# Round three of a graph network: each tile finished inside the loop of sums

## The chip, the cores and the metric

The kernel runs on one core of a Trainium2 chip. The metric is the device time of one execution in microseconds (us), smaller is better. The core has a matrix engine (PE; its weight loads are listed as PEld), a vector engine (DVE), a scalar engine (ACT), a general engine that here issues gathers and scatters (POOL) and a queue engine that issues DMA transfers (SP). Each engine works through its own list of instructions in order; between engines, semaphores make an instruction wait for what it reads.

## The reference, cut to what matters

A residual network of eight layers acts on 3125 nodes with 256 features. Each layer adds its output to x, and each reads the layer norm of x. The change lies in the third round, a weighted graph convolution with a two-layer product behind it, and in the preparation of the mixture layer that follows, whose gate is an attention over another graph of 65536 edges:

```python
# round three, graph layer (sums over the first graph, self-loops included)
xw = layernorm(x) @ W
h7 = segment_sum(xw[col] * (dinv[row] * ew * dinv[col])[:, None], row) + b
x = x + relu(h7 @ W1 + b1) @ W2 + b2
# round three, mixture layer: scores of the gate, over the other graph
h = layernorm(x) @ W_gat                      # 4 heads of 4 values
a_src, a_dst = (h * att_src).sum(-1), (h * att_dst).sum(-1)
# attention over the other graph's edges, norm, the best 2 of 4 experts
...
x = x + sum over experts of gate * (gelu(layernorm(x) @ W1[e] + b1[e]) @ W2[e] + b2[e])
```

## The kernel before

The nodes are 25 tiles of 128 rows (`T` = 25, `D` = 256, `DC` = 2 halves of the features, `TG` = 5 tiles to a group). The rounds follow one another; this document is about the stretch from the end of round two's mixture to the first gather of round three's attention.

`r2_gnn` (L1010) norms all tiles, transposes them (`moe_input`, L672, `tr_ps`), multiplies by W and scales by `dv` (`r_p`, `r_xw`), then calls `src_sum` (L2334). That is the loop this document calls **the loop of sums**. In its iteration t one matrix `ss_wt` of 1.6 MB is loaded from memory and 25 products are summed in `ss_sum` for tile t (L2360; each f32 product is two PE instructions, so 50 instructions). Beside the sums, the loop puts the other graph's edges in order, block by block. `own_order` (L1791) is a generator with five steps; the steps of block b are called here S1 to S5:

- S1: ACT makes a one-hot matrix `oo_h` (17 Abs, L1801, and one Relu, L1802).
- S2: DVE adds it up and scans it (`oo_hs`, `oo_sm`, `oo_ls`).
- S3: PE makes two small products (`oo_p`, L1826, L1827); DVE works out places (`oo_m`, `oo_pos`, `oo_eq`, `oo_pi`, `oo_pf`, L1831 to L1849); ACT makes a second one-hot `oo_hp` from `oo_pf` (again 17 Abs and a Relu); DVE makes `oo_hk`, `oo_rh` (L1855, L1859).
- S4: PE multiplies `oo_hp` with `oo_rh` (L1864, 17 instructions).
- S5: DVE writes the ordered block into `own_gi` and `own_rel` (L1867 to L1869).

Iteration t runs S1(t), S3(t-1), S4(t-2), the sums of tile t, S5(t-2), `done(t-1)` (two DVE operations on `r_acc`, L1040, L1041), S2(t). All of it stands under `self.in_order(nc.tensor, nc.vector, nc.scalar)` (L1920): PE, DVE and ACT each execute their instructions of the loop strictly in the order in which the program emits them. SP, POOL and everything outside such a block are ordered by the planner.

After the loop, `own_marks` (L1872) marks first and last edges for all 25 blocks at once (`mark_edges`, L1628: per block a copy, a PE transpose and a cast, then four transposes and transfers into `relT`); all 25 `r_acc` tiles are transposed; the two-layer product runs over four tiles at a time (`r_a`, L1058, Relu on ACT, `r_o`, L1065) and is added to `self.X` with the bias b2 (L1067, L1068). Then `r2_ffn` (L2367) loads the gate's weights (`head_weights`, L1905), norms x (`norm_group`, L145), transposes it (`tr_ps`), multiplies by the gate's weights (`q_hp`, L2409), copies (`q_hx`, L2411) and writes the rows `q_rows` to memory; the attention's POOL gathers (`ad_rows`, L322) read them.

Of the kernel before, what the change touches and what calls it, by code (L numbers as in the profile page):

```python
# [36 lines left out]
NP = T * P  # L37
D = 256
DC = D // P
# [4 lines left out]
TG = 5  # L44
# [1113 lines left out]
class Fast(Net):  # L1158
# [469 lines left out]
    def mark_edges(self, s, first, pool, p2, psp):  # L1628

        nc, K = self.nc, s.K  # L1630
        nc.vector.tensor_scalar(s.neg, s.rel, float(P), -BIG, op0=OP.is_ge, op1=OP.mult)
# [3 lines left out]
        for k in s.k0:  # L1635
            nc.vector.memset(go[:, k:k + 1], 0.0)
        st = pool.tile([P, K], F32, name="te_st")
        nc.vector.tensor_tensor_scan(st, go, first, 0.0, OP.mult, OP.max)
        nc.vector.tensor_scalar_mul(s.cum, st, -BIG)
        nc.vector.tensor_scalar(go, go, -1.0, 1.0, op0=OP.mult, op1=OP.add)  # L1640
        nc.vector.tensor_max(go, go, first)
        nc.vector.tensor_scalar_mul(s.drop, go, -BIG)
# [8 lines left out]
        for k in range(0, K, W):  # L1651
            ps = psp.tile([P, P], F32, name="te_pr")[0:W, :]
            nc.tensor.transpose(ps, s.rel[:, k:k + W], self.ident)
            r = p2.tile([W, P], BF16, name="te_r")
            nc.vector.tensor_copy(r, ps)
            nc.sync.dma_start(s.relT[k:k + W, :], r)
# [90 lines left out]
    def own_load(self):  # L1747
# [6 lines left out]
        self.edge_tiles(s, keep, "own", self.d.rec.rearrange("p k f -> p (k f)"))  # L1754
        s.low = keep.tile([P, KB, KB], BF16, name="own_low")
# [116 lines left out]
    def own_marks(self):  # L1872

        nc, tc, s = self.nc, self.tc, self.o
        K = s.K
        with tc.tile_pool(name="om", bufs=1) as pool, tc.tile_pool(name="om2", bufs=2) as p2, \
                tc.tile_pool(name="om_ps", bufs=2, space=PSUM) as psp:
            n = KB * (T - 1)
            ends = pool.tile([P, 2, T], F32, name="om_ends")
            full = s.rel1[:, 0:n].rearrange("p (d k) -> p d k", k=KB)  # L1880
            for i, (u, v) in enumerate(((KB - 1, KL - 1), (0, 0))):
                nc.vector.tensor_copy(ends[:, i, 0:T - 1], full[:, :, u])
                nc.vector.tensor_copy(ends[:, i, T - 1:T], s.rel1[:, n + v:n + v + 1])
            near = pool.tile([P, 2, P], F32, name="om_near")
            nc.vector.memset(near, 0.0)
            nc.vector.tensor_copy(near[:, 0, 1:P], self.ident[:, 0:P - 1])
            nc.vector.tensor_copy(near[:, 1, 0:P - 1], self.ident[:, 1:P])
            first = pool.tile([P, K], F32, name="om_first")
            ps = psp.tile([P, 2, T], F32, name="om_p")
            for i in range(2):  # L1890
                nc.tensor.matmul(ps[:, i, :], near[:, i, :], ends[:, i, :], start=True, stop=True)
            r, f, l = s.rel1, first, s.last
            nc.vector.tensor_tensor(f[:, 1:K], r[:, 1:K], r[:, 0:K - 1], OP.not_equal)
            nc.vector.tensor_tensor(l[:, 0:K - 1], r[:, 0:K - 1], r[:, 1:K], OP.not_equal)
            nc.vector.tensor_tensor(f[:, 0:n].rearrange("p (d k) -> p d k", k=KB)[:, :, 0], full[:, :, 0], ps[:, 0, 0:T - 1], OP.not_equal)
            nc.vector.tensor_tensor(l[:, 0:n].rearrange("p (d k) -> p d k", k=KB)[:, :, KB - 1], full[:, :, KB - 1],
                                    ps[:, 1, 0:T - 1], OP.not_equal)
            nc.vector.tensor_tensor(f[:, n:n + 1], r[:, n:n + 1], ps[:, 0, T - 1:T], OP.not_equal)
            nc.vector.tensor_tensor(l[:, K - 1:K], r[:, K - 1:K], ps[:, 1, T - 1:T], OP.not_equal)
            no = pool.tile([P, K], F32, name="om_no")  # L1900
            nc.vector.tensor_scalar(no, r, 0.0, 256.0, op0=OP.is_equal, op1=OP.mult)
            nc.vector.scalar_tensor_tensor(s.rel, r, -1.0, no, op0=OP.add, op1=OP.add)
            self.mark_edges(s, first, pool, p2, psp)
# [430 lines left out]
    def src_sum(self, rows, done):  # L2334


        nc, tc = self.nc, self.tc
        self.own_load()
        with tc.tile_pool(name="ss_w", bufs=2) as wp, tc.tile_pool(name="ss_ps", bufs=2, space=PSUM) as psp, \
                tc.tile_pool(name="oo", bufs=2) as op, tc.tile_pool(name="oo1", bufs=1) as o1, \  # L2340
                tc.tile_pool(name="oo_ps", bufs=1, space=PSUM) as osp, \
                self.in_order(nc.tensor, nc.vector, nc.scalar):
            ways, sums = {}, {}

            def step(b):
                if b in ways:
                    next(ways[b])

            for t in range(T + 2):
                if t < T:  # L2350
                    ways[t] = self.own_order(t, op, o1, osp)
                step(t)
                step(t - 1)
                step(t - 2)
                if t < T:
                    wt = wp.tile([P, T, P], F32, name="ss_wt")
                    nc.sync.dma_start(wt, self.mats[:, t, :, :])
                    sums[t] = psp.tile([P, D], F32, name="ss_sum")
                    for d in range(T):
                        nc.tensor.matmul(sums[t], wt[:, d, :], rows[:, d, :], start=d == 0, stop=d == T - 1)  # L2360
                step(t - 2)
                if t - 1 in sums:
                    done(t - 1, sums[t - 1])
                step(t)
        self.own_marks()

    def r2_ffn(self):  # L2367
# [7 lines left out]
        with ExitStack() as ctx:  # L2375
            pool = ctx.enter_context(tc.tile_pool(name="q", bufs=1))
# [17 lines left out]
            for e in range(1, E):  # L2394
                nc.vector.memset(early[:, e, 0:e], 1.0)
            we = self.head_weights(pool, a["L2_ffn_W_gat"], a["L2_ffn_att_src"].rearrange("h c -> (h c)"),
                                   a["L2_ffn_att_dst"].rearrange("h c -> (h c)"), C=4)
            xT = self.moe_input(pool)
            hx = pool.tile([P, T, Q + 4], F32, name="q_hx")
            ad = pool.tile([P, T, 4], F32, name="q_ad")  # L2400
            sf = pool.tile([P, T, 4], F32, name="q_sf")
            rows = self.dram.tile([NP, Q + 4], F32, name="q_rows")
            with tc.tile_pool(name="q_ps", bufs=2, space=PSUM) as psp:
                for g in range(0, T, TG):
                    gs = slice(g, g + TG)
# [166 lines left out]
```

## Time and profile before

| | us |
|---|---|
| median of 3 runs | 5167.04 (5164.95 to 5167.39) |
| profiled execution, its time | 5171.12 |
| profiled execution, its span | 5169.1 |
| busy in the span: PE, DVE, ACT, POOL | 3584.2, 2916.1, 2087.0, 2063.2 |
| first product of the loop of sums to the last tile's sums | 2690.93 to about 3049 |
| first gather of round three's attention | 3217.24 |

The page of the profile lists busy times of each engine, the chain of work that ended last, and groups of instructions with their mean durations. Times inside the span are counted from its start. A line of a timeline gives start, duration, engine, source line, operation, output and inputs, how many instructions were merged, and in brackets how long the engine sat idle before it and what released it.

### The profile page before, as it was taken

The page shows a single profiled execution, that of the slowest core. Times are in us where ns is not written, and L with a number is a line of the kernel's source. Part 1 is how long each engine was busy: PE and PEld are TensorE (multiplying, and loading weights), DVE is VectorE, ACT ScalarE, POOL GpSimd, SP SyncE. Part 2 cuts the span into 40 slices and gives each one's busy share as a digit, 9 for nine tenths or more (in the row PEclk, how much of TensorE's full clock was granted, in tenths as well). Part 3 has the DMA queues.
Part 4 walks back from the last instruction along what each step waited for, and adds up shares of the span by engine and source line. Part 5 has one row for each costly group of instructions (what it writes and reads, how often), then busy time and mean ns, then how long its engine had stood idle before and what let it go on. Part 6 is the DMA issues. An engine that isn't in the chain of part 4 may idle for free.

```text
span 5169.1 us, 67040 instructions
## 1 busy us (share of the span) xinstructions
PE 3584.2 (69%) x21332; PEld 2847.3 (55%) x21332; DVE 2916.1 (56%) x9571; ACT 2087.0 (40%) x5715; POOL 2063.2 (40%) x2082
## 2 busy tenths in 40 slices
PE   1399969625666354554648876168786999979994
PEld 1399958524444243443537754035554788868883
DVE  7998842255666466663358874577747872231112
ACT  3466432116666467661129961023232331112220
POOL 0365443467776677775620000777700000120003
PEclk9699979866777677777969986578887999989997
DMA  1632237534554344434723311111100112225554
GB/s 55 206 109 103 99 123 234 174 89 136 142 142 125 97 133 130 135 99 132 205 74 115 115 57 45 34 31 35 33 1 25 68 68 76 92 103 193 193 192 135
DMA packets 345199, 562.37 MB, mean 109 GB/s; under 512 B 69987, under 2 KB 255719, under 8 KB 341637
## 3 DMA queue, kind: packets, MB, share of 16 engines
q1 hardware_dynamic: 229050, 373.88, 21.8%
q0 software_dynamic: 84032, 154.27, 11.7%
q10 hardware_dynamic: 31754, 29.84, 1.7%
q8 instruction: 172, 2.82, 0.2%
q14 instruction: 191, 1.56, 0.1%
HBM read 412.89 MB, written 145.37 MB: 108 GB/s over the span
## 4 chain that ended last, share of the span: by engine, by line
PE 44%; POOL 11%; DVE 9%; ACT 9%; issue 8%; DMA 5%; SPq 1%; DVEq 0%; ACTq 0%; POOLq 0%
POOL ad_rows L322 9%; PE gx_pa L962 7%; PE r_pa L1581 7%; PE gx_po L933 7%; PE ad_acc L2133 6%; ACT oo_y L1801 4%; PE q_a L2484 3%; PE q_o L2492 3%; PE r_o L1596 2%; DMA ad_rows<-r_rows,fa_gi 1%; DMA gb_y<-ff_results,gd_at 1%; ACT ad_rows L2123 1%; ACT oo_hp L1802 1%; ACT oo_h L1802 1%; DMA gx_xs<-regions 1%
## 5 line engine op out<-in xcount | busy, mean ns | idle before, releaser
L322 POOL DMA_INDIRECT ad_rows<-r_rows,fa_gi x832 | 823.3, 990 | 266.4 <-issue 241.3
L1737 POOL DMA_INDIRECT os_table<-os_rec,os_at x512 | 531.1, 1037 | 526.2 <-ACT gx_h L963 194.0
L322 POOL DMA_INDIRECT ad_rows<-q_rows,own_gi x416 | 402.6, 968 | 719.9 <-DMA q_rows<-q_hx 593.4
L2123 ACT ACTIVATE ad_rows<-ad_rows 128x64 f32<-128x64 f32 x2544 | 617.0, 334 | 1.6
L2133 PE MATMUL ad_acc<-ad_rows,ad_hd 128*128 128x260 f32 x1664 | 515.9, 464 | 3.3 <-ACT ad_rows L2123 2.4
L831 POOL DMA_INDIRECT regions<-gh_xn,gd_at x150 | 157.5, 1050 | 845.7 <-PE r_o L1596 624.4
L1581 PE MATMUL r_pa<-r_xs,r_cnt 128*128 128x257 bf16 x3750 | 467.7, 277 | 28.1 <-DVE r_xs L1357 14.2
L963 ACT ACTIVATE gx_h<-gx_pa,gx_bias 128x256 f32<-128x256 f32 x448 | 211.9, 473 | 671.2 <-PE gx_pa L962 642.6
L935 DVE TENSOR_TENSOR gx_ys<-gx_po,gx_b 128x256 f32<-128x256 f32 x192 | 80.6, 423 | 622.1 <-PE gx_po L933 600.8
L962 PE MATMUL gx_pa<-gx_xt,gx_w 128*128 128x256 f32 x1792 | 418.5, 388 | 6.8 <-DMA gx_w<-in_L_ffn_W 3.2
L933 PE MATMUL gx_po<-gx_w,gx_h 128*128 128x256 f32 x1792 | 419.5, 380 | 0.0
L1581 PEld LDWEIGHTS <-r_cnt 128*128 128x128 bf16 x3750 | 365.0, 99 | 84.9 <-issue 29.4
L2133 PEld LDWEIGHTS ad_acc<-ad_rows,ad_hd 128*128 128x128 f32 x1664 | 365.8, 232 | 68.9 <-ACT ad_rows L2123 5.4
L2036 PE MATMUL ad_pt<-ident,ad_e 128*4 128x128 f32 x75 | 26.6, 354 | 525.9 <-DVE ad_e L2033 396.0
L962 PEld LDWEIGHTS gx_pa<-gx_xt,gx_w 128*128 128x128 f32 x1792 | 336.6, 192 | 81.7 <-DVE gx_xt L957 21.5
L933 PEld LDWEIGHTS gx_po<-gx_w,gx_h 128*128 128x128 f32 x1792 | 331.2, 190 | 44.0 <-ACT gx_h L963 2.6
L322 POOL DMA_INDIRECT gb_y<-ff_results,gd_at x150 | 144.3, 962 | 526.9 <-DMA ff_results<-gx_ys 476.1
L2036 PEld LDWEIGHTS ad_pt<-ident,ad_e 128*4 128x4 f32 x75 | 6.1, 82 | 559.1 <-issue 527.4
L1462 PE MATMUL r_pa<-r_xn,r_wt 128*128 128x257 f32 x1250 | 298.1, 383 | 7.2 <-ACT r_wt L1497 5.9
L2360 PE MATMUL ss_sum<-r_xw,ss_wt 128*128 128x256 f32 x1250 | 292.0, 396 | 6.3 <-DMA ss_wt<-mats 6.3
L2360 PEld LDWEIGHTS ss_sum<-r_xw,ss_wt 128*128 128x128 f32 x1250 | 246.9, 199 | 42.3 <-issue 6.7
L1462 PEld LDWEIGHTS r_pa<-r_xn,r_wt 128*128 128x128 f32 x1250 | 228.4, 192 | 35.5 <-ACT r_wt L1497 6.5
(555 smaller groups left out, 6920.6 us busy)
## 6 DMA issues: line engine op xcount, KB each, us to landing
gx_w<-in_L_ffn_W SPq DMA_DIRECT2D x64, 1024.0 KB
mats<-r_wt SPq DMA_DIRECT2D x25, 1600.0 KB
ss_wt<-mats SPq DMA_DIRECT2D x25, 1600.0 KB
gx_w<-in_L_ffn_W SPq DMA_DIRECT2D x64, 512.0 KB
regions<-zero SPq DMA_DIRECT2D x26, 1024.0 KB
ad_rb<-fa_relT SPq DMA_DIRECT2D x48, 544.0 KB
gx_xs<-regions SPq DMA_DIRECT2D x96, 256.0 KB
ff_results<-gx_ys ACTq DMA_DIRECT2D x96, 256.0 KB
```

Of the source, the lines that this page charges most:

```text
L322: return self.nc.gpsimd.indirect_dma_start(out=out, out_offset=None, in_=table[:, :], in_offset=bass.IndirectOffsetOnAxis(ap=idx, axis=0))
L831: ins = nc.gpsimd.indirect_dma_start(out=self.regions[:, :], out_offset=bass.IndirectOffsetOnAxis(ap=m.at[i][:, t:t + 1], axis=0), in_=x, ...
L933: nc.tensor.matmul(po, h[:, f, j * P:(j + 1) * P], w2s[:, f, :], start=f == 0, stop=f == FC - 1)
L962: nc.tensor.matmul(ps, w1s[:, c, f * P:(f + 1) * P], xt[:, c, :], start=c == 0, stop=c == DC - 1)
L963: done = nc.scalar.activation(h[:, f, :], ps, act, bias=bias1[:, f, k:k + 1])
L1462: nc.tensor.matmul(pa, wt[:, i, :], xn[:, g * G + i, :], start=i == 0, stop=i == G - 1)
L1581: nc.tensor.matmul(pa, c[:, u, :], xs[i - 1][:, u, j, :], start=u == 0 and j == 0, stop=u == T - 1 and j == 2)
L1737: i = nc.gpsimd.indirect_dma_start(out=s.table[:, :], out_offset=bass.IndirectOffsetOnAxis(ap=s.at[:, c:c + 1], axis=0), in_=s.rec[:, c, : ...
L1801: nc.scalar.activation(y[:, k, :], self.iotab, AF.Abs, bias=minus[:, k:k + 1])
L2123: i = nc.scalar.activation(v, v, AF.Copy, scale=x.rt[:, k, W4 + h:W4 + h + 1])
L2133: nc.tensor.matmul(x.acc, lhs[:, k, :], rhs[:, k, :], start=i == 0, stop=i == x.kb - 1)
L2360: nc.tensor.matmul(sums[t], wt[:, d, :], rows[:, d, :], start=d == 0, stop=d == T - 1)
```

## The change

`src_sum` is merged into a new `r2_gnn`. Behind the sums of a tile, the rest of that tile's work is put into the same loop, under the same fixed order, as generators in a list `later`; `on()` moves each of them one step, in list order. It is called twice in an iteration: before the sums of tile t and behind them. In this document the steps are F1, F2, F3 for `finish` (transposes and copy; first product and Relu; second product and add), M1 and M2 for `own_marks` of five blocks, and N, B1, B2, B3, Q for `scores` of five tiles (norm; three batches of transposes; scores, copy and transfer; its first step is empty).

The loop's new PSUM tiles are: `te_pr` in one buffer (marks), `lt_pt` in two (all transposes and the first product), `lt_po` in one (the second product and the scores). The start of the round also changes: tile by tile it transposes, copies on ACT, multiplies by W and scales; the gate's weights are loaded there; b2 is added to X by 25 POOL operations. `r2_ffn` loses its norm, transposes and scores.

```diff
-    def mark_edges(self, s, first, pool, p2, psp):
+    def mark_edges(self, s, first, pool, p2, psp, b0=0, b1=T):
...
-        for b in range(T):
+        for b in range(b0, b1):
             e = p2.tile([P, 4], F32, name="te_e")
             k = s.k0[b] + s.kb[b] - 1
             nc.vector.tensor_copy(e, s.cum[:, k:k + 1].to_broadcast([P, 4]))
...
             nc.tensor.transpose(ps, e, self.ident)
             nc.vector.tensor_copy(s.dropT[:, b, :], ps)
...
-    def own_marks(self):
+    def own_marks(self, pool, p2, psp, near, b0, b1):
...
+        for i, (u, v) in enumerate(((KB - 1, KL - 1), (0, 0))):
+            nc.vector.tensor_copy(ends[:, i, 0:full], wide[:, :, u])
...
+        for i in range(2):
+            nc.tensor.matmul(ps[:, i, 0:n], near[:, i, :], ends[:, i, 0:n], start=True, stop=True)
+        nc.vector.tensor_tensor(f[:, 1:K], r[:, 1:K], r[:, 0:K - 1], OP.not_equal)
...
+        yield
+        self.mark_edges(s, f, pool, p2, psp, b0, b1)
...
+                for g in range(0, T, TG):
+                    xn = xp.tile([P, TG, D], F32, name="r2_xn")
+                    self.norm_group(lp, xn, g)
+                    for t in range(TG):
...
+                        nc.scalar.copy(xt, pt)
...
+                            nc.tensor.matmul(ps, xt[:, c, :], w[:, c, :], start=c == 0, stop=c == DC - 1)
+                        nc.vector.tensor_scalar_mul(xw[:, g + t, :], ps, dv[:, g + t:g + t + 1])
+                    for t in range(g, g + TG):
+                        nc.gpsimd.tensor_add(self.X[:, t, :], self.X[:, t, :], b2)
...
+                    tc.tile_pool(name="om_ps", bufs=1, space=PSUM) as mps, \
...
+                    tc.tile_pool(name="lt_ps", bufs=2, space=PSUM) as bank, \
+                    tc.tile_pool(name="lt_po", bufs=1, space=PSUM) as one, \
+                    self.in_order(nc.tensor, nc.vector, nc.scalar):
...
+                def finish(t, total):
+                    acc = tp.tile([P, D], F32, name="lt_acc")
+                    nc.vector.tensor_add(acc, total, xw[:, t, :])
+                    nc.vector.scalar_tensor_tensor(acc, acc, dv[:, t:t + 1], b, op0=OP.mult, op1=OP.add)
+                    yield
...
+                        nc.tensor.transpose(pt[:, c, :], acc[:, c * P:(c + 1) * P], self.ident)
+                    at = tp.tile([P, DC, P], F32, name="lt_at")
+                    nc.scalar.copy(at, pt)
+                    yield
...
+                            nc.tensor.matmul(ph[:, f, :], w1[:, c, f * P:(f + 1) * P], at[:, c, :], start=c == 0, stop=c == DC - 1)
+                    for f in range(DC):
+                        nc.scalar.activation(h[:, f, :], ph[:, f, :], AF.Relu, bias=b1[:, f:f + 1])
+                    yield
+                    po = one.tile([P, D], F32, name="lt_po")
+                    for f in range(DC):
+                        nc.tensor.matmul(po, h[:, f, :], w2[:, f, :], start=f == 0, stop=f == DC - 1)
+                    nc.vector.tensor_add(self.X[:, t, :], self.X[:, t, :], po)
+                    if t % TG == TG - 1:
+                        later.append(scores(t + 1 - TG))
...
+                def scores(g):
+                    gs = slice(g, g + TG)
+                    yield
+                    xn = lp.tile([P, TG, D], F32, name="lt_xn")
+                    self.norm_group(lp, xn, g)
+                    yield
...
+                    for u, v in ((0, 2), (2, 4), (4, 5)):
...
+                                nc.tensor.transpose(pt[:, c, t - u, :], xn[:, t, c * P:(c + 1) * P], self.ident)
+                        nc.scalar.copy(q.xT[:, :, (g + u) * P:(g + v) * P].rearrange("p c (t n) -> p c t n", n=P), pt[:, :, 0:v - u, :])
+                        yield
+                    ps = one.tile([P, D], F32, name="lt_po")[:, 0:TG * (Q + 8)].rearrange("p (t w) -> p t w", t=TG)
...
+                            nc.tensor.matmul(ps[:, t, :], q.xT[:, c, (g + t) * P:(g + t + 1) * P], q.we[:, c, :],
+                                             start=c == 0, stop=c == DC - 1)
+                    nc.scalar.copy(q.hx[:, gs, :], ps[:, :, 0:Q + 4])
+                    nc.sync.dma_start(q.rows[g * P:(g + TG) * P, :].rearrange("(t p) w -> p t w", p=P), q.hx[:, gs, :])
+                    nc.vector.tensor_copy(q.ad[:, gs, :], ps[:, :, Q + 4:Q + 8])
...
+                for t in range(T + 2):
+                    if t < T:
+                        ways[t] = self.own_order(t, op, o1, osp)
+                    step(t)
+                    step(t - 1)
+                    step(t - 2)
+                    on()
+                    if t < T:
+                        wt = wp.tile([P, T, P], F32, name="ss_wt")
+                        nc.sync.dma_start(wt, self.mats[:, t, :, :])
+                        sums[t] = psp.tile([P, D], F32, name="ss_sum")
+                        for d in range(T):
+                            nc.tensor.matmul(sums[t], wt[:, d, :], xw[:, d, :], start=d == 0, stop=d == T - 1)
+                    step(t - 2)
+                    on()
+                    if t - 1 in sums:
+                        way = finish(t - 1, sums[t - 1])
+                        next(way)
+                        later.append(way)
+                    step(t)
+                    if t >= 2 and (t - 2) % TG == TG - 1:
+                        later.append(self.own_marks(mp, mp2, mps, near, t - 1 - TG, t - 1))
+                while later:
+                    on()
```

More of the change, by code (lines that the diff above doesn't have):

```diff
@@ L1870, in own_order @@
         yield
-    def own_marks(self):
[L1874 to L1903, printed above, removed]
@@ L2330, in middle @@
             self.r1_ffn()
[L2334 to L2365, printed above, removed]
@@ L2395, in r2_ffn @@
                 nc.vector.memset(early[:, e, 0:e], 1.0)
[L2396 to L2405, printed above, removed]
-                    ps = psp.tile([P, TG, Q + 8], F32, name="q_hp")
-                    for t in range(TG):
-                        for c in range(DC):
-                            nc.tensor.matmul(ps[:, t, :], xT[:, c, (g + t) * P:(g + t + 1) * P], we[:, c, :],
-                                             start=c == 0, stop=c == DC - 1)
-                    nc.scalar.copy(hx[:, gs, :], ps[:, :, 0:Q + 4])
-                    nc.sync.dma_start(rows[g * P:(g + TG) * P, :].rearrange("(t p) w -> p t w", p=P), hx[:, gs, :])
-                    nc.vector.tensor_copy(ad[:, gs, :], ps[:, :, Q + 4:Q + 8])
-                nc.vector.tensor_add(sf, hx[:, :, Q:Q + 4], ad)
-                nc.vector.scalar_tensor_tensor(sf, sf, 0.2, sf, op0=OP.mult, op1=OP.max)
             ag = pool.tile([P, T, Q], F32, name="q_ag")
```

130 lines of the change are left out of this document (117 added, 13 removed).

## The prediction

> **What bounds the kernel now.** I read the page first, then the busy time by stage, then the timeline of one iteration. In the windows below the columns are window, length, then busy time (and count) of PE, PEld, DVE, ACT, POOL, then PE clock, DMA share, GB/s. They are, in order: start of the round, loop of sums, marks, transposes of the sums, two-layer product, weights and norm, scores.
>
> ```profile
> 2626.00:2691.00 65.00, 39.10 (x151) 27.21 (x151) 45.41 (x128) 23.16 (x56) 0.00 (x0) 0.68 0.11 38
> 2691.00:3050.00 359.00, 307.46 (x1691) 261.85 (x1691) 288.71 (x621) 333.60 (x837) 0.00 (x0) 0.95 0.30 109
> 3050.00:3081.00 31.00, 11.24 (x60) 4.67 (x61) 25.98 (x139) 3.98 (x10) 0.00 (x0) 0.57 0.09 24
> 3081.00:3098.00 17.00, 14.48 (x51) 8.23 (x50) 7.92 (x21) 4.84 (x13) 0.00 (x0) 0.50 0.01 3
> 3098.00:3145.00 47.00, 46.37 (x156) 28.99 (x154) 13.53 (x33) 8.98 (x14) 0.00 (x0) 0.96 0.00 1
> 3145.00:3192.00 47.00, 14.64 (x50) 7.86 (x50) 33.90 (x68) 11.37 (x22) 0.00 (x0) 0.51 0.34 103
> 3192.00:3218.00 26.00, 21.50 (x100) 21.41 (x100) 4.83 (x26) 2.49 (x6) 0.76 (x1) 0.50 0.15 32
> ```
>
> The loop is 93% ACT, 86% PE, 80% DVE; the five stages behind it, 168 us from 3049 to the first gather at 3217, use one engine at a time. That is what the change fills. One iteration, by engine:
>
> ```profile
> 2878.59 5.08 ACT L1801 ACTIVATE oo_y<-iotab,own_rel 128x128 bf16<-128x128 bf16 x17
> 2883.70 2.11 ACT L1802 ACTIVATE oo_h<-oo_y,ones 128x2176 bf16<-128x2176 bf16 x1
> 2885.84 5.07 ACT L1801 ACTIVATE oo_y<-iotab,oo_pf 128x128 bf16<-128x128 bf16 x17
> ```
> ```profile
> 2878.61 0.62 PE L1864 MATMUL oo_p<-oo_rh,oo_hp 128*128 128x51 bf16 x17 [2.81 <-ACT oo_hp L1802]
> 2879.08 12.72 PE L2360 MATMUL ss_sum<-r_xw,ss_wt 128*128 128x256 f32 x50
> ...
> 2893.57 11.04 PE L2360 MATMUL ss_sum<-r_xw,ss_wt 128*128 128x256 f32 x50
> ```
> ```profile
> 2882.97 0.18 DVE L1849 TENSOR_SCALAR oo_pf<-oo_pi 128x17 f32<-128x17 int32 x1
> ...
> 2883.89 1.06 DVE L1859 TENSOR_TENSOR oo_rh<-oo_hk,own_f 128x867 bf16<-128x867 bf16 x1
> ...
> 2891.95 1.22 DVE L1831 TENSOR_TENSOR oo_m<-oo_h,oo_p 128x1024 f32<-128x1024 bf16 x1 [3.40 <-PE oo_p L1827]
> ```
>
> ACT has no gap: S1 and S3's one-hot are 7.25 each, so a tile is 14.5. PE waits 2.8 for `oo_hp`, DVE 3.4 for `oo_p`; both waits lie beside ACT. From `oo_p` DVE starts 0.38 later, reaches `oo_pf` after 7.3 more and `oo_rh` after 9.0. The sums take 11.04, or 12.72 in a granted clock that fell during a pause. In the tail:
>
> ```profile
> 3140.33 0.38 PE L1058 MATMUL r_a<-xT,r_W 128*128 128x128 f32 x2
> ...
> 3142.41 0.83 PE L1058 MATMUL r_a<-xT,r_W 128*128 128x128 f32 x6
> ```
> ```profile
> 3213.77 0.24 ACT L2411 COPY q_hx<-q_hp 128x100 f32<-128x100 f32 x1 [4.02 <-PE q_hp L2409]
> ```
> ```profile
> 3217.24 0.94 POOL L322 DMA_INDIRECT ad_rows<-q_rows,own_gi  x1 [593.44 <-DMA q_rows<-q_hx]
> ```
>
> The first product over 128 columns, as F2 has it, costs 0.38 + 0.83 = 1.2; from `q_hx` to the first gather 3.5.
>
> **An ordinary iteration after.** Order under the fixed list, iteration t: ACT S1(t), S3(t-1), F1's copy (t-2), F2's Relu (t-2); PE `oo_p`(t-1), S4(t-2), F3(t-3), F1(t-2), sums(t), F2(t-2); DVE S3(t-1), F3's add, S5, acc, S2(t). Let e be the end of F2 on PE. ACT: two Relu 0.75 (row of `r_ht` 128x128) and S1 end at e+8.15; `oo_pf` is there at e+7.7, hidden; the one-hot ends at e+15.4, F1's copy (0.37, row of `xT`) at e+15.8. PE: 0.1 + 0.5 + 0.9 (F3) + 0.5 (F1) + 11.04 ends at e+13.5, at the low clock e+15.2, and waits for that copy; F2 ends at e+17.1. So a tile takes 17.1: ACT's 14.5 + 0.4 + 0.8, and 1.4 in which ACT waits for the product between its own copy and its own Relu.
>
> **What each group of five adds**, in iterations 7 to 10, 12 to 15, and so on:
>
> - M1 puts PE's small product with `near` ahead of the sums, and its input behind S3 and F3's add on DVE. So the sums, queued behind it on PE, start not at e+2 but at e+10.8 (0.4 + 9.0 + 0.45 + two copies 0.45 + 0.5). With 12.7 after the pause and F2's 1.2, e moves 24.7 instead of 17.1: +7.6.
> - M2 sits on DVE ahead of acc and S2. Its five transposes stand behind the sums and F2 on PE, in one PSUM buffer: copy 0.15, transpose 0.45, cast 0.25 per block, 4.0, and 0.8 for `relT`. Then acc 0.85, S2 2.45, `oo_p` 0.4: S3 starts at e+8.4, `oo_pf` is at 15.7, the one-hot ends at 23.0 (15.4 before).
> - N stands ahead of F1's copy on ACT: Square 1.3 to 24.3, DVE's variance 1.75 to 26.05, Sqrt 0.3, DVE's 0.7 + 1.5 to 28.6; then B1's transposes 1.2 and F2 1.2: 31.0, with M2's delay +13.9.
> - B2 and B3: copies of 0.7 and 0.4 on ACT, 0.6 from handing over: +1.7.
> - Q's scores and the next F3 share the one `lt_po` buffer. It is freed by `q_hx`, which stands behind the one-hot on ACT: e+15.7. F3, F1 and the sums wait behind it on PE: 15.7 + 0.9 + 0.5 + 11.04 (to 13.4, the row of the first sums after 6.3 idle) + 1.2 = 29.4 to 31.7: +13.
>
> DVE's operations of the group (norm 7.1, marks 6 in all) fall into DVE's pauses otherwise; if that cover went, 2.6 a tile. Transfers: `relT` and `q_rows` join SP's queue, where the load of `ss_wt` two tiles ahead is ready earlier; I take 0. Were a load queued behind `q_rows` instead, it would cost up to 6.2 (the wait for the first `ss_wt`) a group.
>
> **The sum.** F2(0) ends at 2735.2 (the one-hot of block 1 ends at 2733.6 before, + 0.4 + 1.2), 44.3 after the first product of the sums. 22 ordinary iterations to iteration 24: 376. Extras: 4 x 7.6 + 4 x 13.9 + 4 x 1.7 + 3 x 13 = 132. So iteration 24 ends 552 after the first product; before, 358.6: the loop costs +194. Behind it: iterations 25 and 26 without sums 16; F3 1.5; last marks 2.2 + 6.8; norm 8.9; transposes 6.2 at the low clock; scores 20 x 0.215 = 4.3 (row of `q_hp`); 3.5 to the gather: 50 where 168 stood, -118. Start of the round: PE's 39.1 in a 65 us window could end 16 earlier when the products by W start before the last norm; the 25 POOL adds have no row (at DVE's 0.41 they are 10, at three times that 31, over 360 us before their tile is needed). Bounds -16 and +10, I take -8. The experts' weights (4 MB, some 21 at 200 GB/s) were loaded under the old norm; their memory is free only near the end now, and `q_rows` may queue behind: 0 to +21, I take +3, since most of it can go during the last marks. Sum: 194 - 118 - 8 + 3 = +71. The profiled execution took 5171.1 (span 5169.1), 4 over the median: 5171 + 71 - 4 = 5238.
>
> About 0.2%, 10 us, is what a measurement of this kernel can tell from no change.
>
> **The rivals.** *Faster: the waits fall beside the work.* For it: over five tiles no engine is full. ACT's addition is 0.4 + 0.8 a tile and 3.8 a group (Square 1.3, Sqrt 0.2, three copies 1.9, `q_hx` 0.25), so 16.4 a tile; PE's comes to about 15.3 (11.04 + 0.7 + 2.6, and 5 a group in transposes and scores), DVE's to 15.8 (12.7 + 0.45 + 2.6). If ACT alone set the pace, the loop would cost 22 x 1.95 + 3 = +46 and the whole -77: 5090. It decides when a cycle of five tiles takes under 101 us: 72.5 before, plus five times the 123 to be won over 22 tiles; I find 5 x 17.1 + 36.2 = 122. Against it: each wait above comes from a fixed order, and PE's and DVE's gaps in the profile show that these engines do stand still for one instruction.
> *The Trainium skill says otherwise:* its page "Perfetto Trace Analysis", section "Identifying the Most-Contended Engine", takes the engine with the highest occupancy as the bottleneck; by that ACT's 93% rules and this rival's number would be the forecast. The trace agrees for the loop of before, where ACT has no gap; whether occupancy still rules after the change no run shows yet.
> *No change:* the waits of M1 and Q are absent because the copies come early: 71 - 30 - 39 = 2, 5169. Against it: `q_hx` is emitted behind S3.
> *Worse:* weights delay `q_rows` by 21, and clock or SP's queue takes 6 a group: 5280.
> *Not what it says:* the last five tiles' marks, norm and scores still follow the loop one after another; that is the 50 counted above, and half of a gather's delay more would show there.
>
> **How the numbers follow.** Slower as summed 0.63 (own range 5200 to 5270), worse 0.10, faster 0.20, no change 0.07. The range 5120 to 5290 reaches below for part of the faster case and leaves out some 0.15 there and 0.04 above. Faster by over 0.2%: 0.2; within: 0.05 (the no-change case spreads a little beyond); slower: 0.75.
>
> **What the profile after would show.** Right: ordinary tiles 17.1 apart, ACT idle 1.3 before the Relu on `lt_h`, released by PE; cycles of five of about 122; PE idle for 8 before the product with `near`, released by DVE, and for 10 or more before an F3, released by ACT's `q_hx`; the first gather near 3288. Wrong: ACT over 95% busy in the loop, tiles at 16.4, first gather near 3140.

## The result and the profile after

The changed kernel takes 5234.81 us (median of 4 runs, 5228.12 to 5235.24) where the kernel before takes 5167.22: ratio 1.0127, 95% interval 1.0109 to 1.0144. The forecast was 5238. The profiled execution took 5228.12, with a span of 5226.3; its granted clock is 0.828 of full speed, against 0.831.

Windows of the changed kernel first; the columns are as in the prediction: window, length, busy time and count of PE, PEld, DVE, ACT and POOL, then PE clock, DMA share and GB/s. The first line is most of the head of the round, the second what lies between the loop and the first gather, the third the loop of sums with the wait for the last scores behind it.

```profile
2626.00:2681.00 55.00, 36.99 (x141) 27.51 (x141) 34.64 (x64) 12.48 (x29) 18.65 (x25) 0.81 0.14 45
...
3236.00:3275.00 39.00, 17.34 (x80) 13.26 (x80) 18.66 (x85) 5.47 (x14) 0.37 (x1) 0.63 0.49 141
2681.00:3236.00 555.00, 409.68 (x2186) 350.40 (x2185) 348.88 (x832) 367.04 (x938) 0.00 (x0) 0.83 0.20 71
```

The window of the loop grew from 359 to 555 (547 without that last wait), and no engine is near full in it: ACT fell from 93% to 66% (367.04 of 555), PE from 86% to 74%, DVE from 80% to 63%. The clock granted to PE fell from 0.95 to 0.83. The five stages of 168 us behind the loop have shrunk to 47. So the time before went into waiting for one engine after another at the end; the time after goes into waiting inside the loop. Who waits for whom, over the loop (engine, line, what it waited for: us in total, times, longest):

```profile
ACT lt_h L2436 <- PE lt_pt L2434: 94.8, 23, 12.9
DVE oo_m L1838 <- PE oo_p L1834: 82.7, 21, 18.8
ACT oo_y L1808 <- DVE oo_pf L1856: 68.0, 9, 28.4
DVE own_dropT L1652 <- PE te_pr L1651: 51.1, 20, 12.2
...
PE lt_po L2440 <- DVE q_ad L2467: 35.4, 3, 12.6
...
PE te_pr L1896 <- DVE om_ends L1890: 29.1, 4, 7.9
...
PE lt_pt L2457 <- DVE lt_xn L170: 24.3, 4, 6.6
...
PE lt_pt L2434 <- ACT lt_at L2428: 18.2, 8, 2.7
...
DVE q_ad L2467 <- ACT q_hx L2465: 17.6, 3, 5.9
```

These are the prediction's waits: Relu behind F2's product, the product by `near` behind `om_ends`, F3 behind the score buffer, F2 behind F1's copy. The second and third lines are S3, which starts late when something ahead of it waits (18.8 and 28.4 of them are one wait each at the start of the loop); the fourth is M2, whose transposes stand behind the sums and F2 on PE. One releaser reads differently from the forecast. PE is shown as released by DVE's `q_ad`, not by ACT's `q_hx`; the last line shows why that is the same wait, since `q_ad` itself stands behind `q_hx`. The single waits on PE's timeline (start, length, instruction, in brackets the idle time before it and its releaser):

```profile
2801.53 1.02 PE L1896 MATMUL te_pr<-om_ends,om_near 128*128 128x5 f32 x4 [7.92 <-DVE om_ends L1890]
2802.41 13.32 PE L2488 MATMUL ss_sum<-r_xw,ss_wt 128*128 128x256 f32 x50
...
2844.69 1.12 PE L2457 MATMUL lt_pt<-ident,lt_xn 128*128 128x128 f32 x4 [6.41 <-DVE lt_xn L170]
2845.60 1.92 PE L2434 MATMUL lt_pt<-lt_at,r_W 128*128 128x128 f32 x8
...
2850.41 10.96 PE L2488 MATMUL ss_sum<-r_xw,ss_wt 128*128 128x256 f32 x50
...
2881.10 2.08 PE L2440 MATMUL lt_po<-r_W,lt_h 128*128 128x256 f32 x4 [10.18 <-DVE q_ad L2467]
```

PE stands for 7.92 ahead of a product of 1.02, and the fifty products of the sums behind it then take 13.32, where they take 10.96 two iterations later. The windows of these two sums show the clock granted to PE beside it, 0.82 and 1.00:

```profile
2802.41:2815.40 12.99, 12.99 (x51) 11.08 (x52) 2.43 (x20) 4.61 (x10) 0.00 (x0) 0.82 0.00 0
2850.41:2861.20 10.79, 10.79 (x52) 9.31 (x50) 10.21 (x25) 9.76 (x28) 0.00 (x0) 1.00 0.01 2
```

So this pause costs itself and a lower clock after it.

Below, an iteration is measured from the start of F2's product on PE to the next one. The length of the loop, here and in the experiments, runs from the first product of the sums to the first `oo_p` on PE behind F2 of iteration 24, which starts as that F2 ends (in the kernel before, to the end of the last sums).

| us | predicted | changed kernel |
|---|---|---|
| ordinary iteration | 17.1 | 16.7 (16.4 to 17.4, 7 of them) |
| with the product by `near` (M1) | 24.7 | 24.8 |
| with the norm (N) | 31.0 | 30.1 |
| with transposes of the scores (B) | 18.8 | 18.5 |
| with the scores (Q) | 30.1 | 30.9 |
| loop, first product of the sums to the end of iteration 24 | 552 | 547.1 |
| from there to the first gather | 50 | 47.0 |

Before, the last two were 358.6 and 167.7. So the loop costs +188.5 and the stretch behind it -120.7, together +67.8; the medians differ by 67.6. The two profiled spans differ by 57.2 only, because round two, whose code is the same, ended 9.5 earlier in that execution (last combine into X at 2616.59 instead of 2626.07). In later runs, all with the same code ahead of it, this point lies anywhere from 2615.8 to 2623.7 on chips where the kernel before takes 5166 to 5167. So I take it for variation between executions; that is not shown, since the kernel before has one profile only, but the medians agree with the sum of the stages without it. The first gather, forecast near 3288, came at 3274.63, which is 3284 with these 9.5 added.

### The profile page after: what moved, and what is told of

Same layout as the page of the kernel before. It is cut to its first block, busy times and chain, and to the rows that moved or that the text cites. A ratio compares the mean times of both kernels' runs of the same rounds, so it can differ in the third digit from the quotient of the medians.

```text
span 5226.3 us, 67476 instructions
## 1 busy us (share of the span) xinstructions
PE 3595.9 (69%) x21493; PEld 2879.5 (55%) x21493; DVE 2910.1 (56%) x9577; ACT 2100.6 (40%) x5779; POOL 2082.2 (40%) x2107
## 4 chain that ended last, share of the span: by engine, by line
PE 52%; DVE 15%; POOL 12%; issue 9%; ACT 7%; DMA 5%; SPq 0%; DVEq 0%; POOLq 0%; ACTq 0%
POOL ad_rows L322 10%; PE gx_pa L962 7%; PE r_pa L1581 7%; PE gx_po L933 7%; PE ad_acc L2140 5%; PE r_pa L1462 5%; PE q_a L2601 3%; PE q_o L2609 3%; ACT oo_y L1808 2%; PE r_pw L1493 2%; PE ss_sum L2488 2%; PE r_o L1596 2%; ACT ad_rows L2130 1%; DMA gb_y<-ff_results,gd_at 1%; DMA ad_rows<-r_rows,fa_gi 1%
## 5 line engine op out<-in xcount | busy, mean ns | idle before, releaser
L1581 PE MATMUL r_pa<-r_xs,r_cnt 128*128 128x257 bf16 x3750 | 468.1, 277 | 28.1 <-DVE r_xs L1357 14.2
```

Of the source, the lines that this page charges most:

```text
L1581: nc.tensor.matmul(pa, c[:, u, :], xs[i - 1][:, u, j, :], start=u == 0 and j == 0, stop=u == T - 1 and j == 2)
```

## The experiments

Two theories were tested. The first is the prediction's: the fixed order of the list makes engines wait for one another, and the place of an operation costs, not its work. The rival is that the busiest engine sets the loop, so an edit that only moves work brings nothing.

The first four kernels ran on a chip on which the kernel before itself takes 5952.29. The stretches ahead of the loop and behind the first gather are longer there: the first product of the sums starts at 3213 to 3228, against 2681 in the changed kernel, and from the first gather to the end it takes 2195 to 2224, against 1952. Their ratios are against that 5952.29; the changed kernel itself did not run there. The loop can be compared across chips all the same: its first five F2 products start at 42.4, 58.8, 76.2, 92.7 and 110.1 after the first product of the sums in the changed kernel, and at 42.7, 59.2, 76.6, 93.0 and 110.4 in the second experiment, which does not touch them. The changed kernel, run a second time on another occasion, gave the same 594.1 to the first gather.

**Marks behind the loop.**

```diff
-                    if t >= 2 and (t - 2) % TG == TG - 1:
-                        later.append(self.own_marks(mp, mp2, mps, near, t - 1 - TG, t - 1))
                 while later:
                     on()
+                for u, v in ((0, 15), (15, T)):
+                    for _ in self.own_marks(mp, mp2, mps, near, u, v):
+                        pass
```

> The marks of the other graph's edges are no longer made inside the loop of sums: all 25 blocks' marks are made behind it, in two calls of 15 and 10 blocks. Theory (waits set by the fixed order): the iterations with the product by `near` fall from 24.8 to about 17, those with the norm from 31.1 to about 23.4 since the five transposes no longer hold back acc and S2: 4 x (7.7 + 7.7) = -62 in the stretch from the first product of the sums to the last F2 of the loop, 547 -> about 485. Behind the loop the marks of 25 blocks take about 31 (the stage in the profile of before) instead of some 9: at most +22. Total 40 to 50 below the changed kernel, about 5190. Rival (an engine's occupancy sets the loop): ACT's work in the loop is untouched, so the loop stays at 547 and the total rises by up to 22, to 5235-5257.

Measured: loop 488.1 (485 expected). The M1 iterations fell from 24.8 to 16.5, those with the norm from 30.1 to 23.3; the Q iterations took 31.5 for 30.9. Ratio to before 1.0026 (1.0014 to 1.0038). The first product of the sums to the first gather fell to 529.7, but the marks now reach behind that gather, at 3742.44: on DVE's timeline their last cast into `own_dropT` stands 97 later, and the 69th gather sat idle for 33.25 before it.

```profile
3839.43 0.28 DVE L1652 CAST own_dropT<-te_pr 4x128 bf16<-4x128 f32 x1 [0.47 <-PE te_pr L1651]
```
```profile
3860.76 1.16 POOL L322 DMA_INDIRECT ad_rows<-q_rows,own_gi  x1 [33.25 <-issue]
```

In the second experiment the same gather waited this long:

```profile
3879.35 1.16 POOL L322 DMA_INDIRECT ad_rows<-q_rows,own_gi  x1 [14.80 <-issue]
```

What released that gather the profile does not say. The stretch behind the first gather took 2224.3, against 2194.9 to 2206.3 in the other three kernels on this chip. So the rival falls: with ACT's work untouched the loop lost 59. That the place of the marks had cost this, and not their work, is shown only further below, where they stay in the loop.

**Scores in the two-buffer pool.**

```diff
-                    ps = one.tile([P, D], F32, name="lt_po")[:, 0:TG * (Q + 8)]...
+                    ps = bank.tile([P, 512], F32, name="lt_pt")[:, 0:TG * (Q + 8)]...
```

> One edit: the scores of a group are summed in a buffer of the pool with two buffers (`lt_pt`) instead of the single `lt_po`. Theory: the product F3 behind the scores no longer waits for `q_hx`, so the three iterations with scores lose their 13 extra; but DVE still stands at `q_ad` until ACT has come through the one-hot to `q_hx`, which delays acc, S2 and the next S3 by about 4. So 3 x (13 - 4) = -27 (bounds -20 and -39): loop 547 -> about 520, total about 5208. Rival (occupancy): no work is removed, 0. A third possibility: the wait only moves to the two-buffer pool, whose next buffer is then awaited by F2: 0 as well, but with PE waiting ahead of the product into `lt_pt`.

Measured: loop 513.7, 33 less (27 expected, bounds 20 and 39); ratio to before 1.0037 (1.0021 to 1.0053). On PE's timeline of this kernel F3 now follows the scores without a gap:

```profile
3405.99 4.44 PE L2463 MATMUL lt_pt<-hw_w,q_xT 128*128 128x24 f32 x20
3410.26 2.05 PE L2440 MATMUL lt_po<-r_W,lt_h 128*128 128x256 f32 x4
```

A Q iteration and the ordinary one after it took 47.3 together and now take 36.5, so they lose 10.8 of the 14.2 that Q had cost above an ordinary iteration (30.9 less 16.7); some 3.4 stay, near the 4 expected, and the gain is larger because Q's extra was 14.2 and not 13. The third possibility, that the wait moves to the pool, is out: PE's waits ahead of F2's product into `lt_pt` for F1's copy come to 17.9 in all, against 18.2 in the changed kernel.

**F1 ahead of S3's one-hot.** S3 of `own_order` gets one more `yield`, just before its one-hot.

```diff
                     step(t - 1)
+                    if fresh:
+                        next(fresh[0])
+                    step(t - 1)
                     step(t - 2)
                     on()
+                    later += fresh
...
```

> One edit: F1's transposes stand ahead of S4 on PE and its copy ahead of S3's one-hot on ACT (before: behind it). The work is the same. Theory: F2's product is ready as soon as the sums end and no longer waits 2.3 to 2.7 for the copy; ordinary tiles go from 16.9 to about 15.6 (7 x 1.3 = 9), tiles with transposes of the scores the same (4 x 1.3 = 5), and in the iterations with the norm the copy no longer stands behind Square and Sqrt, 4 x 5 = 20; those with scores gain some 1 each: about -37, total about 5198. Rival (occupancy): 0.

Measured: loop 522.8, 24 less (37 expected); ratio to before 1.0053 (1.0034 to 1.0071). On ACT's timeline of this kernel the copy stands between the two one-hots, with no wait on either side:

```profile
3310.28 2.11 ACT L1809 ACTIVATE oo_h<-oo_y,ones 128x2176 bf16<-128x2176 bf16 x1
3312.29 0.35 ACT L2429 COPY lt_at<-lt_pt 128x256 f32<-128x256 f32 x1
3312.55 5.10 ACT L1808 ACTIVATE oo_y<-iotab,oo_pf 128x128 bf16<-128x128 bf16 x17
```

Ordinary iterations fell to between 13.4 and 15.1, more than expected: with the earlier first F2 they give 19 instead of 9. B and Q iterations did not change (8 expected). Those with the norm fell from 30.1 to 25.5, 18 in all, but M1 iterations rose from 24.8 to 28.1, 13 in all, so the two together gave 5, where the norm's alone were to give 20. PE's timeline shows both reasons. In this kernel `finish` comes into the list behind the marks, so F2 stands behind M2's transposes, and their 3.7 now count in the M1 iteration:

```profile
3342.09 0.27 PE L1651 MATMUL te_pr<-ident,te_e 128*4 128x128 f32 x1
...
3345.78 1.06 PE L2435 MATMUL lt_pt<-lt_at,r_W 128*128 128x128 f32 x8
...
3370.36 1.11 PE L2458 MATMUL lt_pt<-ident,lt_xn 128*128 128x128 f32 x4 [5.87 <-DVE lt_xn L170]
3371.26 1.91 PE L2435 MATMUL lt_pt<-lt_at,r_W 128*128 128x128 f32 x8
```

In the changed kernel F2 stood ahead of them:

```profile
2815.56 1.05 PE L2434 MATMUL lt_pt<-lt_at,r_W 128*128 128x128 f32 x8
2816.45 0.27 PE L1651 MATMUL te_pr<-ident,te_e 128*4 128x128 f32 x1
```

And in the iteration with the norm, F2 still stands behind B1's transposes, which wait 5.87 for the norm's scaling, as they waited 6.41 before: the earlier copy cannot help there. The wait ahead of the product by `near` did not grow (6.37, where it was 7.92). Taking one wait away helps only where no other wait stands ahead of the same instruction.

**The norm in five steps.** Mean and subtraction, Square, variance, Sqrt and scaling are separated by `yield`s; Square and Sqrt run ahead of S3's one-hot.

```diff
-                    self.norm_group(lp, xn, g)
...
+                    nc.vector.tensor_tensor(xn, x, m[:, :, None].to_broadcast([P, TG, D]), OP.subtract)
+                    yield "C"
...
+                    nc.scalar.activation(sq, xn, AF.Square)
+                    yield "B"
...
+                    nc.vector.tensor_reduce(v, sq, AX.X, OP.add)
...
+                    yield "C"
...
+                    nc.scalar.activation(r, v, AF.Sqrt)
+                    yield "B"
...
```

> One edit: the norm of a group is cut into five steps put at different places of the loop (mean and subtraction; Square ahead of S3's one-hot; variance; Sqrt ahead of the next one-hot; scaling), so that neither ACT nor DVE stands while the other works at the same norm. The transposes and scores of the group come two iterations later than before; the work is the same. Theory: the iterations with the norm fall from 31.1 to about 25 (the delay by the marks' transposes stays), 4 x 6 = -24, total about 5211; bounds -16 and -32. The steps behind the loop are the same chain: 0. Rival (occupancy): 0.

Measured: loop 517.1, 30 less (24 expected, 16 to 32); ratio to before 1.0045 (1.0027 to 1.0062). The size is right for a partly wrong reason. The iterations with the norm fell only from 30.1 to 26.8, which is 13 in all. The other 17 came from the later place of the transposes and scores: the four B iterations fell from 18.5 to 16.5, and Q now falls into the iteration of the next group's M1. Both waits together take 34.6, and the iteration that Q has left 16.5 to 17.5, where the two took 24.8 and 30.9.

**Marks in the loop, in six steps.** The marks stay in the loop, with DVE's and PE's parts a place apart; four of the five blocks' transposes go into one bank and are cast at once.

```diff
         for i, (u, v) in enumerate(((KB - 1, KL - 1), (0, 0))):
             ...
+        yield "B"
         ...
             nc.tensor.matmul(ps[:, i, 0:n], near[:, i, :], ends[:, i, 0:n], start=True, stop=True)
+        yield "C"
         nc.vector.tensor_tensor(f[:, 1:K], r[:, 1:K], r[:, 0:K - 1], OP.not_equal)
         ...
-        self.mark_edges(s, f, pool, p2, psp, b0, b1)
...
+        yield "B"
+        for i in range(n - 1):
+            nc.tensor.transpose(ps[0:4, i * P:(i + 1) * P], e[:, i, :], self.ident)
+        yield "C"
+        nc.vector.tensor_copy(s.dropT[:, b0:b1 - 1, :], ...)
...
```

> One edit: the marks of a group stay in the loop but are cut into six steps, each where its input is ready (DVE's `om_ends` after S3; the product by `near` behind the sums; DVE's work after the next S3; four transposes behind the sums into one bank; one cast after the next S3; the last two transposes behind the sums, their casts after the next S3). Theory: it is the place of the marks and not their work that costs: the loop falls as with the marks behind it, 547 -> about 488 (to 500), and nothing comes back later: first product to first gather 594 -> about 540. Rival: the marks' 3 to 6 of DVE and 2 of PE a group take their time wherever they stand: the loop falls by less than half of that, to 520 or more.

Measured: loop 489.9 (488 to 500 expected), to the first gather 532.5 (540 expected), total 5167.62 against 5166.02 of the kernel before: ratio 1.0002 (0.9993 to 1.0011). This edit alone takes back the change's whole loss. The same product by `near` on PE's timeline of this kernel:

```profile
2815.18 0.86 PE L1898 MATMUL te_pr<-om_ends,om_near 128*128 128x5 f32 x4
```

No idle time stands before it now. The loop is within 2 of the one without any marks (488.1), so it is their place and not their work that cost: the rival, 520 or more, falls.

**The bias adds of the head left out.** POOL's 25 adds are missing, so X lacks that bias.

```diff
-                    for t in range(g, g + TG):
-                        nc.gpsimd.tensor_add(self.X[:, t, :], self.X[:, t, :], b2)
```

> The 25 POOL adds of the second layer's bias to X are left out (X lacks that bias from here on). Theory A: they lengthen small DVE operations beside them (0.64 to 0.82 instead of 0.17 in the profile after), some 4.9 in all, and that is why the head won 0.9 and not 8: from the last combine of round two to the first product of the sums 63.5-64.4 -> about 59. Theory B: DVE's own list (norms, scalings of the products by W, the first S2, own_load) sets the head, with the norm's buffers freed by PE: 63 to 64 as now.

Measured, from the end of the last combine of round two to the first product of the sums: 57.7, against 61.7 to 62.5 in the three kernels with the adds that ran on the same chip (61.7 to 64.4 over all). Theory A holds, with 4 to 5; this is one profile, but the last kernel below, whose head has no adds either, shows 58.0. The loop is unchanged (547.1). The first of POOL's adds in the changed kernel, three DVE instructions beside the adds, then the same three without them:

```profile
2629.01 11.73 POOL L2401 TENSOR_TENSOR X<-X,r_b 128x256 f32<-128x256 f32 x15 [15.06 <-DMA r_b<-in_L_gnn_b]
```
```profile
2638.09 0.64 DVE L163 TENSOR_SCALAR ln_v<-ln_v 128x5 f32<-128x5 f32 x1
2638.64 0.77 DVE L156 TENSOR_SCALAR ln_m<-ln_m 128x5 f32<-128x5 f32 x1
2639.32 0.82 DVE L1824 TENSOR_TENSOR oo_sm<-oo_hs 128x128 bf16<-128x128 bf16 x1
```
```profile
2636.68 0.16 DVE L163 TENSOR_SCALAR ln_v<-ln_v 128x5 f32<-128x5 f32 x1
2636.74 0.16 DVE L156 TENSOR_SCALAR ln_m<-ln_m 128x5 f32<-128x5 f32 x1
2636.82 0.22 DVE L1824 TENSOR_TENSOR oo_sm<-oo_hs 128x128 bf16<-128x128 bf16 x1
```

**The changed kernel again.**

> The changed kernel once more, beside the others: first product to first gather 594, loop 547, head 63.5 to 64.4, as in its first profile; about 68 more than the kernel before in whatever total this chip gives.

Measured: 594.1, 547.1 and 61.7, so the head lies below the 63.5 to 64.4 expected and varies by some 3 between executions; 5233.31 us, ratio to before 1.0130 (1.0115 to 1.0146).

**All steps placed.** The edits above together (marks, norm, F1, scores), with F3 and the copies of the scores' transposes also ahead of S3's one-hot:

```diff
                     step(t)
                     step(t - 1)
+                    on("C")
+                    step(t - 1)
                     step(t - 2)
-                    on()
                     ...
                     step(t - 2)
-                    on()
+                    on("B")
```

> All steps of the tiles, marks, norms and scores are placed by one rule: an operation stands in the list at a place where its input is ready when its engine gets there. F3 and F1 stand ahead of S4 on PE, F1's copy, Square, Sqrt, the copies of the scores' transposes and `q_hx` ahead of S3's one-hot on ACT; the marks are cut into five steps, the norm into five, the scores into a two-buffer pool with their copy one place later. The work is the same but for the marks' casts (four blocks in one). Theory (waits of the fixed order): no engine waits for another in most iterations; ACT's 14.5 + 0.35 + 0.63 and PE's 11.0 + 1.2 + 0.8 + 1.1 + 0.7, with the group's share, make some 15.5 to 16 a tile: loop 547 -> about 415 (400 to 440), first product of the sums to the first gather 594 -> about 465, about 60 under the 526 of the kernel before: ratio to before about 0.988 to 0.99. Rival (the group's work itself has no room on three engines that were 93, 86 and 80% busy): the waits only move, loop about 500, ratio about 1.004.

Measured: loop 396.3 (415 expected, at least 400), to the first gather 435.5 (465 expected), total 5072.36: ratio to before 0.9818 (0.9805 to 0.9832). The forecast was too careful, and the rival, a loop of about 500, falls again: the group's work has room.

**DVE's part of the marks two iterations later.** On top of the last kernel, two more `yield "C"` behind the product by `near`.

> On top of the kernel with all steps placed (first product to first gather 435.5): DVE's 3.7 of the marks stands two iterations later, no longer in the same iteration as the norm's variance (1.65). In the profile of that kernel this iteration took 20.7 and the others 14.6 to 16, with PE idle 4.4 ahead of `oo_p`, released by DVE's `oo_ls`. Theory (a full DVE holds back S2 in that one iteration): 20.7 -> about 17, four times, less what comes back in the other: loop 396 -> about 384 (380 to 390), total about 12 less. Rival (ACT and PE are full on average, the wait is made up by the short iterations of 14.6): 396 as now.

Measured: loop 384.0 as expected (382.9 to the end of F2 itself; PE waits 1.1 for `oo_p` there), to the first gather 423.5, total 5061.20: ratio to before 0.9791 (0.9775 to 0.9808). The loop of this kernel in the busy time by window, and the largest waits in it:

```profile
2685.00:3068.00 383.00, 354.32 (x2131) 312.30 (x2131) 333.52 (x777) 355.34 (x924) 0.00 (x0) 0.98 0.28 103
```
```profile
DVE oo_m L1838 <- PE oo_p L1834: 38.8, 24, 18.8
ACT oo_y L1808 <- DVE oo_pf L1856: 33.2, 5, 28.4
PE oo_p L1833 <- DVE oo_ls L1829: 16.6, 11, 2.1
...
PE lt_po L2473 <- ACT lt_h L2469: 10.0, 10, 1.3
```

28.4 of the second line is one wait at the start of the loop, where the kernel before has one of 39.4. ACT is at 93% again, PE at 93%, DVE at 87%, and PE's clock at 0.98. PE's busy time is 354.32, against 409.68 in the changed kernel's window.

**Bias adds one by one in the loop.** On top of that, POOL's adds leave the head, and each stands behind DVE's add of F3.

```diff
                     nc.vector.tensor_add(self.X[:, t, :], self.X[:, t, :], po)
+                    nc.gpsimd.tensor_add(self.X[:, t, :], self.X[:, t, :], b2)
```

> On top of that: POOL's 25 adds of the bias stand no longer beside the norms of the head but one by one behind DVE's add of F3 in the loop. Theory: the head falls from 62 to 64 to about 58, as without the adds, and the loop pays less than it wins, since one add of 0.7 a tile lengthens one or two small DVE operations: total about 3 to 5 less than without this edit. Rival: DVE is the busiest in the loop, each add delays it by 0.5 to 1: 25 x 0.5 = 12 comes back there, total up to 8 more.

Measured: head 58.0, as expected, but first product of the sums to first gather 428.9, so 5.4 come back in the loop and behind it. Total 5057.61, ratio to before 0.9787 (0.9771 to 0.9803). The median is 3.6 lower, but the two kernels' times overlap (5055.76 to 5060.54 and 5054.80 to 5064.29): no difference that these runs can tell.

## Why the prediction was right, step by step

**The loop**, +194 forecast, +188.5 measured. For the marks, the score buffer and F1's copy the mechanism is shown, not only argued: the wait ahead of each vanished when its place was changed while its work stayed. For the norm the wait shrank. M1 with M2's transposes is worth 57 to 59 of the loop, the score buffer 33, F1's copy 24 and the norm with its later transposes and scores 30, of which 13 (4 x 3.3) lie in the iterations with the norm. The parts overlap, since Q and M1 in one iteration cost less than in two. So the sum of extras in the prediction holds for this order alone. That the single edits add up to 144 to 146, near the 151 of all steps placed, proves nothing about adding them, since that kernel also moved F3 and copies.

**The terms.** Ordinary iterations measured 16.7 for 17.1. The wait between F1's copy and F2's Relu was 1.25 where F2 took 1.16 and 2.17 where it took 2.07, and the two kinds alternate at first; 1.4 was taken for all. Without that wait 15.2 are left of the iteration, where the prediction added up 15.7 on ACT; so its sum of ACT's work was 0.5 too large. The norm's iteration was 0.9 shorter than forecast, Q's 0.8 longer. Over the loop the ordinary part came some 9 lower than forecast and the extras some 4 higher, so these errors cancel in part. These two lines of ACT show the ordinary wait:

```profile
2790.24 0.35 ACT L2428 COPY lt_at<-lt_pt 128x256 f32<-128x256 f32 x1
2791.84 0.63 ACT L2436 ACTIVATE lt_h<-lt_pt,r_b 128x128 f32<-128x128 f32 x2 [1.25 <-PE lt_pt L2434]
```

**Behind the loop**, -118 forecast, -120.7 measured.

**The head**, -8 forecast: this term was mis-sized. It was 64.4 before and is 61.7 to 64.4 with the change and the adds, so 0 to -3. The products by W do start earlier, but they no longer follow the norms: they take turns with them on DVE. The last scaling of the norm ended 23 after the last combine before the change and 48 after it in the changed kernel. The prediction counted POOL's adds as POOL's time alone and not for what they do to DVE; leaving them out brought 4 to 5. Without them the head is 57.7, 6.7 under the kernel before; the last 1.3 were not tested.

Here a rule of the Trainium skill can be set behind the rows. Its page "SBUF — State Buffer", section "SBUF: two separate sides", says that VectorE and GpSimd share one pair of ports, which goes for a whole instruction to whichever starts first: a GpSimd operation, or a VectorE operation that runs in a two-port mode or has two SBUF inputs (the latter only against a GpSimd operation that reads SBUF). The trace agrees in part: of eleven small DVE operations on SBUF that overlap an add, nine took 0.51 to 0.82, instead of 0.14 to 0.22 without the adds, and two were not longer (0.16 and 0.28). The adds take 0.69 to 0.78 each on average. Scalings read from PSUM stayed at 0.48 and a reduction of 1280 at 1.48. Of two DVE operations with two SBUF inputs of 1280, one took 1.97 beside an add instead of 1.49, the other stayed at 1.49. In which mode DVE's small operations run, no run here shows.

**The experts' weights**, +3 forecast (0 to 21): from the first gather to the end 1951.7 in the changed kernel's profile (1953.9 in its second) against 1951.8. Nothing to be seen; with that, and with a loop shorter than forecast, the rival "worse" falls.

**The total.** The forecast of +71 was nearer to the measured +67.6 than some of its parts: the loop came 5.5 lower and the stretch behind it 2.7 lower than forecast, the weights 3 lower, the head 5 to 8 higher. That these cancel is luck; the two large terms are not.

**The rival "faster"**, 5090, was not what this order gives, but it was no phantom. Its condition, a cycle of five iterations under 101, is met when the steps are placed: 120.9 in the changed kernel (122 forecast), 81.9 with all steps placed, 78.9 with the marks later, and 5061 in total. The Trainium skill's page "Perfetto Trace Analysis", section "Identifying the Most-Contended Engine", takes the engine with the highest occupancy for the bottleneck, which fits the loop before, where ACT waits once at the start and then has no gap. In the kernel with the marks later ACT and PE stand level (355.34 and 354.32 of 383), and no run here shows which of them binds. In the changed kernel the fullest engine is at 74%, and occupancy does not tell what sets the pace; there the waits had to be read one by one.

## What to carry to other kernels

Where a list fixes each engine's order, work put into another engine's gaps is free only if its input is ready when the engine reaches it. In this kernel it was enough to put a producer and its consumer one place of the list apart, with other work between them, and not to put a short product whose input comes late ahead of a long one. Price the wait of each new instruction against what stands behind it on its queue, buffers with one copy included. If every engine falls well below full after such a change, try to move its steps before undoing it: nearly the same work, placed, took this kernel from 1.3% slower (ratio 1.0127, 1.0109 to 1.0144) to 2.1% faster (0.9791, 0.9775 to 0.9808).

## What the hardware showed that was not expected

A pause of PE costs more than its length. The fifty products of a sum took 10.96 at a granted clock of 1.00 and 13.32 at 0.82 after a pause of 7.9, F2's eight from 1.05 to 2.07. From the first product of the sums to the end of F2 of iteration 24, PE was busy for 404.60 at a mean clock of 0.84 in the changed kernel:

```profile
2681.00:3228.00 547.00, 404.60 (x2152) 345.44 (x2152) 344.12 (x818) 363.06 (x928) 0.00 (x0) 0.84 0.20 72
```

With the marks later it was busy for 354.32 at a clock of 0.98 (2131 records, a little less work). So up to 50 of the loop's difference of 163 between these two kernels stand on PE as busy time, though they go with the waiting. The clock was not varied by itself in any run.

POOL's adds on SBUF made most operations of 5 elements on DVE that fell beside them about four times as long (0.64 instead of 0.16), and that time counts as busy time of DVE. And the kernel before took 5167 on one chip and 5952 on another, while the first five F2 products of the loop, in kernels with the same code up to there, started within 0.4 of each other on the two; the length of a stage in the trace was the safer measure there.
